# First half's routing and tables inside the last chunk of a scan

## The chip, the cores and the metric

The kernel runs on one core of one Trainium2 chip. The metric is the device time in microseconds of one execution; less is better. Engines are named as in the profile: PE is TensorE (matmuls), PEld its weight loads, DVE VectorE, ACT ScalarE, POOL GpSimd, SP the engine whose queue issues most DMA transfers. Each engine works through its own instructions in their order.

## What is computed

The program is a network of two layers over N = 4096 tokens (rows) with D = 256 features; each layer is a graph step with a residual and then a mixture of experts with a residual. The change touches layer 0 only:

```python
# layer 0, graph step: propagation, layer norm, a Mamba block
h = relu(adj @ layernorm(x) @ gcn_w + gcn_b);  h = layernorm(h) * ln_g + ln_b
xz = h @ w_in;  xc, z = xz[:, :512], xz[:, 512:]
u = silu(causal_conv4(xc));  dt = softplus(...);  B, C = ...   # from u @ w_xp
hst = exp(dt * A) * hst + dt * B * u          # scan over the 4096 tokens, 16 states
y = (hst @ C + u * D_skip) * silu(z)
x = x + y @ w_out
# layer 0, experts: 8 experts of 256 -> 512 -> 256, the two best of each token
n = layernorm(x);  probs = softmax(n @ gate_w + gate_b);  top2 of probs
x = x + sum over the two of  prob * (gelu(n @ W1[e] + b1[e]) @ W2[e] + b2[e])
```

Layer 1 is another graph step and another mixture of experts (6 experts, three matmuls each); its code is the same before and after.

## The kernel before

**The scan.** The tokens are cut into NC = 8 chunks of 512. A chunk is scanned in STEPS = 32 steps; a step works on one block of 128 of the 512 inner channels (`m`) and two of the 16 states. A `Step` does this: POOL multiplies `db` (L1138), ACT makes the two decays `da` with Exp (L1154), DVE runs two scans (L1161) and the product `hc` (L1171), PE adds `hc` into the PSUM tile `psy` (L1188), and after the eighth step of a block DVE multiplies `psy` by the gate (L1197, `us`). The `da` tiles lie in PSUM. The order of the work on PE, DVE, ACT and POOL is written out by hand, within `tc.manual_schedule`: one loop over n = 0 to 255, with chunk c and step i, lists what stands at each step. Each engine therefore works strictly in the order of this loop.

**What is filled in between the steps.** The propagation and the front (projection, convolution, dt) of later chunks fill PE in earlier chunks. In the last two chunks the finished chunks are closed:

- A `Tail` is a half chunk of `y @ w_out + x`: `product(0)` and `product(1)` on PE (L929, L933), `put` (a copy on ACT with row sums, L938, and a store to DRAM, `x1d`), and in the following step `squares` on ACT (L948, L952). `Tail.step` does one such piece at each step, from step 8 of chunk 6.
- A `Norm` is a chunk's layer norm: `root` (POOL's pow, L968), `shift` on DVE (L974), then a fetch, `normal` on ACT with stores to `d_xd` and, for the first four chunks, `xd0`, the transposes (`turn`), the matmuls with `gate_w` (`logits`) and `keep`, which puts the router's logits into `lgs`. The tables `NORMS` and `NPIECES` give the step of the last chunk at which each stands: chunk c's `normal` is at step 10 + 3c.
- `Last` is the last chunk's own tail. Half of its w_out products, the residual and the two banks `ps_out` are begun at steps 22 to 28; the rest (L1063) follows the last gate, and then `norm` (L1077 to L1112) does the statistics, the pow, the normal, the stores, the transposes (L1097), the logits (L1104) and the copies `xr` (L1110).

**Routing.** `dp` is the dispatch of layer 0. The tokens are routed in blocks: b = 0 is the first half (chunks 0 to 3), b = 1 and b = 2 are the rest. `choose` calls `router` (L110 to L138: softmax and the best two, 18 operations on DVE and an Exp on ACT). `place` counts with two matmuls (L231, L235) and turns the counts into row numbers on DVE (L240 to L266). `one_hot` writes comparisons of 128 x 1024 (L273). `Part.tables` then builds the tables of a part: a head of small operations (L311 to L351), pairs `tb_eq` (L359, L364 on DVE, L363 on ACT), 32 products on PE into `ps_inv` (L369), and from these, on DVE, which token lies in which row (`d0f_src`, L381 to L387), which expert a tile has (`d0f_exps`, L389) and the biases (`d0f_b`, L395, L400).

**Expert tiles.** Rows are worked off in tiles of 256 rows of one expert. `part0[0]` has FIRST0 = 9 tiles with rows of the first half of the tokens only; `part0[1]` has the other 26. For a tile, `expert_tiles` gathers rows by two indirect DMAs on POOL (L430, `xk`), loads the expert's weights through SP (`wk`, L532, and `bk`, L535), transposes on PE (L539, `ps_xt`), copies (L543, `xkT`), does the first layer (L518, `ps_h`), the Gelu on ACT (L522), the second layer of the tile before it (L503, `ps_y`), and writes the rows back. `others` is a generator with the routing of blocks 1 and 2 and the tables of the second part; `then0(n)` takes pieces of it after tile n.

**The passage from scan to tiles.** After the last step the loop's end reads, in order: the remaining sums, the last gates, the last additions of `Last`, then

```python
        dp.lo = onehots
        dp.choose(0, lgs[:, :dp.T[0], :], gate_b, False, ra)
        dp.place(0, ps_y, "psy", ra)
        last.norm()
```

and after the pools have been changed

```python
            b1 = load(wp, a["L0_ffn_b1"], "b1")
            dp.one_hot(0)
            for _ in part0[0].tables(inverse(), rp, [b1], NT):
                pass
```

Both blocks stand outside `manual_schedule`; there the order on an engine is that of a scheduler. In the trace before, DVE's router operations on the first half lie between the last chunk's late steps, although they are written after them. The one-hots lie in the first half of `gn`, a large SBUF tile whose rows are not needed at that time.

Of the kernel before, what the change touches and what calls it, by code (L numbers as in the profile page):

```python
# [30 lines left out]
def kernel(ctx: ExitStack, tc: tile.TileContext, out: bass.AP, **a):  # L31
# [73 lines left out]
    def router(ps, bias_b, E, rev, renorm, oh, wv, pool):  # L105
# [4 lines left out]
        nc.vector.tensor_tensor(lg, ps, bias_b.unsqueeze(1).to_broadcast([P, T, E]), ALU.add)  # L110
# [8 lines left out]
        nc.scalar.activation(lg, lg, AF.Exp)  # L119
        nc.vector.tensor_reduce(col(1), lg, AX.X, ALU.add)  # L120
# [6 lines left out]
        for i in range(2):  # L127
# [6 lines left out]
            if i == 0:  # L134
                nc.vector.scalar_tensor_tensor(lg, hots[0], -4.0, p, ALU.mult, ALU.add)
                q = lg
        if not renorm:
# [25 lines left out]
    class Dispatch:  # L163
# [47 lines left out]
        def choose(self, b, logits, bias_b, renorm, pool):  # L211
            T, t0 = self.T[b], self.t0[b]
            hots = self.oh[b][:, 1:, :].rearrange("p (t i) e -> p t i e", i=2)
            router(
                logits, bias_b, self.E, self.rev[:, :T, :], renorm, hots,
                self.wv[:, t0:t0 + T, :], pool,
            )

        def place(self, b, psum, tag, pool):

# [6 lines left out]
            if (2 * G + 1) * E <= CW:  # L227
                tot = ps[:, G * E:]
            else:
                tot = psum.tile([P, CW], F32, name="ps_pl1", tag=tag)  # L230
# [6 lines left out]
            )  # L237
            flat = pool.tile([P, E * (G + 1)], F32, name=f"pl_at{G}")
# [15 lines left out]
            )  # L254
            row = pool.tile([P, G], F32, name=f"pl_row{G}")
# [13 lines left out]
        def one_hot(self, b):  # L269

            g0, G, S, row = 2 * self.t0[b], 2 * self.T[b], 2 * TPC, self.row.pop(b)
            for g in range(0, G, S):
# [3 lines left out]
                )  # L276

    class Part:
# [14 lines left out]
        def tables(self, ps, tp, biases, NG, other=None, hots=None):  # L293
# [4 lines left out]
            if hots is None:  # L298
                def hots(shape):
                    return tp.tile(list(shape), BF16, name="tb_eq", bufs=3)  # L300
# [52 lines left out]
            S = 2 * TPC  # L353
            group = dp.group.rearrange("p t i -> p (t i)")
            slots = slot.rearrange("p f h -> p (f h)").unsqueeze(1).to_broadcast([P, S, C])
            for g0 in range(0, NG, S):
# [11 lines left out]
                for g in range(S):  # L368
                    nc.tensor.matmul(  # L369
                        ps[:, :2 * C], dp.lo[:, g0 + g, :], eq[:, :2, g, :],  # L370
                        start=(g0 + g == 0), stop=(g0 + g == NG - 1),
                    )
# [121 lines left out]
    def expert_tiles(jobs, psum, pool, weights, bias_out, layers, kb_out, also=None):  # L494
# [16 lines left out]
        def layer(w, xT, mb, func, bias, name):  # L511
            hT = pool.tile([P, mb, TR], F32, name=name)
            for mm in range(mb // 2):
                ps = ps_h.tile([P, 2, TR], F32, name="ps_h")
                for j in range(2):
                    m = 2 * mm + j
                    for d in range(DB):
                        nc.tensor.matmul(  # L518
                            ps[:, j, :], w[:, d, m * P:(m + 1) * P], xT[:, d, :],
                            start=(d == 0), stop=(d == DB - 1),  # L520
                        )
                    nc.scalar.activation(hT[:, m, :], ps[:, j, :], func, bias=bias[:, m])  # L522
            return hT

        def tile_of(dp, k, prev):
            e = dp.expert(k)
            xk = pool.tile([P, 2, D], F32, name="xk", bufs=4)
            dp.fetch(k, xk)
# [8 lines left out]
            for d in range(DB):  # L537
                for j in range(2):
                    nc.tensor.transpose(  # L539
                        ps[:, d, j * P:(j + 1) * P], xk[:, j, d * P:(d + 1) * P], ident  # L540
                    )
            hT = pool.tile([P, DB, TR], F32, name="xkT")
            nc.vector.tensor_copy(hT, ps)  # L543
# [6 lines left out]
        prev = None  # L550
# [35 lines left out]
    onehots = gn[:, :NT // 2, :].bitcast(BF16).rearrange("p a (b c) -> p (a b) c", c=P)  # L586
    early = ExitStack()
    ra = early.enter_context(tc.tile_pool(name="route0a", bufs=1, side="right"))
    with ExitStack() as s1:
# [430 lines left out]
        SLOW = 3  # L1020
        NORMS, NPIECES = {}, {}
        for i, c0, c1 in ((1, 0, 3), (13, 3, 5), (19, 5, 6), (25, 6, 7)):
            NORMS[i] = lambda s0=c0 * TPC, n=(c1 - c0) * TPC: Norm.root(s0, n)
            NORMS[i + 1] = lambda s0=c0 * TPC, n=(c1 - c0) * TPC: Norm.shift(s0, n)
        for c in range(NC - 1):
            nm = Norm(c)
            for d, piece in (
                (-2, nm.fetch), (0, nm.normal), (1, nm.turn), (2, nm.logits), (3, nm.keep)
            ):
                NPIECES.setdefault(10 + 3 * c + d, []).append(piece)  # L1030

        class Last:
# [13 lines left out]
            def first(self, hh):  # L1046

                self.ps[hh] = (ps_pt, ps_a)[hh].tile(
                    [P, 2, D], F32, name=f"ps_out{hh}", tag=("pt", "d2")[hh]
# [18 lines left out]
            def norm(self):  # L1068
# [3 lines left out]
                xn, xT = [], []  # L1072
                ps_l = ps_m.tile([P, TPC, E0], F32, name="ps_lg", tag="m1")
                for hh in range(2):
# [11 lines left out]
                    for j in range(2):  # L1086
                        nc.scalar.activation(
# [3 lines left out]
                    nc.sync.dma_start(tokens(dp.xd, c)[:, t0:t0 + 2, :], xn[:, :2, :])  # L1091
                    ps_t = (ps_m if hh == 0 else ps_a).tile(
                        [P, DB, HW], F32, name="ps_xnT7", tag=("m0", "d0")[hh]
                    )
                    for k in range(DB):
                        for j in range(2):
                            nc.tensor.transpose(  # L1097
                                ps_t[:, k, j * P:(j + 1) * P], xn[:, j, k * P:(k + 1) * P], ident
                            )
                    xT = w1p.tile([P, DB, HW], F32, name="xnT7", tag=("h", "hT")[hh])  # L1100
                    nc.scalar.copy(xT, ps_t)
                    for j in range(2):
                        for k in range(DB):
                            nc.tensor.matmul(  # L1104
                                ps_l[:, t0 + j, :], xT[:, k, j * P:(j + 1) * P], gate_w[:, k, :],
                                start=(k == 0), stop=(k == DB - 1),
                            )
                    done = nc.scalar.copy(lgs[:, s0:s0 + 2, :], ps_l[:, t0:t0 + 2, :])
                for hh in range(2):
                    after(nc.scalar.copy(self.xr[hh], self.ps[hh]), done)  # L1110
                    rows = tokens(x1d[c], 0)[:, 2 * hh:2 * hh + 2, :]
                    nc.sync.dma_start(rows, self.xr[hh])  # L1112

        class Step:
# [28 lines left out]
            def decay(self, j):  # L1143
# [4 lines left out]
                if not last or tag != "d2":  # L1148
# [50 lines left out]
        with tc.manual_schedule(engines={  # L1199
# [73 lines left out]
            advance(left)  # L1273
            steps, tails, kept, gated, summed, owed = [], [], {}, [], 0, 0
            for n in range(NC * STEPS):
# [46 lines left out]
                Tail.step(tails)  # L1322
                if c == NC - 1:
# [7 lines left out]
                    elif i == 25:  # L1331
                        last.first(0)
                    elif i in (27, 28):
                        last.residual(i - 27)
# [460 lines left out]
```

## Time and profile before

| | us |
|---|---|
| three runs | 2400.75, 2398.1, 2402.75 |
| median | 2400.75 |
| profiled execution | 2412.49 |
| its span, first to last instruction | 2410.7 |
| PE busy | 2239.3 (93%) |
| DVE busy | 1648.1 (68%) |
| ACT busy | 1194.8 (50%) |
| last chunk: end of its first hc to end of its last hc | 1108.19 to 1246.86 |
| last w_out addition ends | 1255.98 |
| first ps_h product of the tiles begins | 1286.92 |

The mean granted TensorE clock was 0.968 of full speed. Times of the profile count from the first instruction of the span. A row of the timeline gives start, duration, engine, line, operation, and in brackets the idle time before it with what ended it ("<-"). Counts of PE records are those of the trace; a float32 matmul leaves more than one.

### The profile page before, as it was taken

How to read it: one execution, taken by the hardware profiler on the slowest of the kernel's cores; microseconds unless marked ns; L12 is line 12 of the kernel's file. 1: busy time of each engine (PE TensorE's matmuls, PEld its weight loads, DVE VectorE, ACT ScalarE, POOL GpSimd, SP SyncE). 2: the span in 40 equal slices, each digit the busy share in tenths (PEclk: the TensorE clock that was granted, in tenths of full speed). 3: DMA queues.
4: the chain of work that ended last, by engine and by line, in shares of the span. 5: the costliest groups of instructions: out<-in, count | busy, mean ns of one | idle time of the engine just before them, and what ended most of it. 6: DMA issues, size and time to landing. Idle time of an engine off the chain costs nothing. (4 is left out here: it accounts for less than half of the span.)

```text
span 2410.7 us, 28097 instructions
## 1 busy us (share of the span) xinstructions
PE 2239.3 (93%) x9018; PEld 1624.2 (67%) x9018; DVE 1648.1 (68%) x2455; ACT 1194.8 (50%) x2050; POOL 1144.8 (47%) x828
## 2 busy tenths in 40 slices
PE   8999999999999999896997999799999999999985
PEld 7665665656465665553666888667888888877774
DVE  2069999999999999998986411291666667742233
ACT  4255666574655666574753322145555555532321
POOL 1057777777877787775644555310000000045652
PEclk9999999999999999998997999999999999999998
DMA  7279999999999999996848877551444444456786
GB/s 237 83 228 227 241 275 238 274 243 268 247 260 258 238 274 238 271 269 174 270 136 266 295 231 228 162 166 53 143 146 148 146 145 146 148 170 209 230 274 235
DMA packets 293071, 511.58 MB, mean 212 GB/s; under 512 B 25376, under 2 KB 159648, under 8 KB 292016
## 3 DMA queue, kind: packets, MB, share of 16 engines
q1 hardware_dynamic: 246640, 412.64, 54.5%
q0 software_dynamic: 46272, 97.03, 18.7%
q8 instruction: 75, 1.23, 0.2%
q14 instruction: 84, 0.69, 0.1%
HBM read 406.03 MB, written 44.83 MB: 187 GB/s over the span
## 5 line engine op out<-in xcount | busy, mean ns | idle before, releaser
L1138 POOL TENSOR_TENSOR db<-du,bb 128x1024 f32<-128x1024 f32 x256 | 607.1, 2372 | 329.5 <-DVE hc L1171 83.1
L1161 DVE TENSOR_TENSOR_SCAN db<-da,state,db 128x512 f32<-128x512 f32 x512 | 627.2, 1266 | 31.5 <-ACT da L1154 29.3
L671 PE MATMUL pt<-at,gn 128*128 128x256 f32 x2048 | 479.4, 387 | 14.9 <-ACT gn L87 9.2
L671 PEld LDWEIGHTS pt<-at,gn 128*128 128x128 f32 x2048 | 397.1, 195 | 135.7 <-issue 63.1
L1154 ACT ACTIVATE da<-dt,negA 128x512 f32<-128x512 f32 x512 | 346.4, 688 | 249.5 <-DVE db L1161 238.7
L1516 PE MATMUL pf<-gn,f 128*128 128x256 f32 x2048 | 452.0, 380 | 0.0
L1516 PEld LDWEIGHTS pf<-gn,f 128*128 128x128 f32 x2048 | 386.6, 190 | 57.2 <-issue 6.4
L1171 DVE TENSOR_TENSOR hc<-db,cb 128x1024 f32<-128x1024 f32 x256 | 328.0, 1281 | 18.2 <-issue 0.4
L1188 PE MATMUL psy<-hc,ident 128*128 128x512 f32 x576 | 301.6, 618 | 4.6 <-DMA hc<-hc 3.7
L81 POOL TENSOR_TENSOR ln_rs<-ln_rs,mhalf 128x4 f32<-128x4 f32 (+1 forms) x25 | 33.4, 1335 | 507.6 <-DVE ln_rs L80 507.1
L508 DVE TENSOR_TENSOR yk<-ps_y,bk 128x512 f32<-128x512 f32 x73 | 50.4, 691 | 308.9 <-PE ps_y L503 232.2
L1505 ACT ACTIVATE f<-f 128x1024 f32<-128x1024 f32 x128 | 134.6, 1057 | 198.7 <-DVE f L1504 128.2
L518 PE MATMUL ps_h<-xkT,wk 128*128 128x256 f32 x864 | 213.6, 388 | 14.7 <-DVE xkT L543 6.9
L503 PE MATMUL ps_y<-wk,hk 128*128 128x256 f32 x864 | 213.3, 382 | 9.2 <-ACT hk L522 6.6
L1175 POOL DMA_DIRECT2D hc<-hc x224 | 195.0, 870 | 0.2
L518 PEld LDWEIGHTS ps_h<-xkT,wk 128*128 128x128 f32 x864 | 159.1, 192 | 50.6 <-ACT hk L522 11.3
L1504 DVE TENSOR_SCALAR f<-at 128x1024 f32<-128x1024 f32 x128 | 88.1, 688 | 148.0 <-PE pf L1516 134.4
L503 PEld LDWEIGHTS ps_y<-wk,hk 128*128 128x128 f32 x864 | 161.9, 191 | 32.7 <-ACT hk L522 8.4
L1188 PEld LDWEIGHTS psy<-hc,ident 128*128 128x128 f32 x576 | 109.3, 196 | 90.2 <-issue 64.0
L1511 DVE SCALAR_TENSOR_TENSOR cnt<-at,cnt 128x1024 bf16<-128x1024 f32 x120 | 145.9, 1216 | 15.9 <-DMA at<-in_adjT_dram 12.3
L1506 ACT ACTIVATE f<-f 128x1024 f32<-128x1024 f32 x128 | 134.5, 1055 | 3.4
L787 PE MATMUL ps_xz<-hT,w_in 128*128 128x512 f32 x256 | 116.3, 597 | 15.2 <-ACT hT L771 8.8
(321 smaller groups left out, 2513.6 us busy)
## 6 DMA issues: line engine op xcount, KB each, us to landing
at<-in_adjT_dram SPq DMA_DIRECT2D x256, 512.0 KB
bb<-bcd SPq DMA_DIRECT2D x128, 512.0 KB
cb<-bcd SPq DMA_DIRECT2D x128, 512.0 KB
hc<-hc POOLq DMA_DIRECT2D x224, 256.0 KB
wk<-in_L_ffn_W_dram SPq DMA_DIRECT2D x70, 512.0 KB
wk<-in_L_ffn_expert_w_dram SPq DMA_DIRECT2D x114, 256.0 KB
yg<-d_ys SPq DMA_DIRECT2D x14, 512.0 KB
yd<-us SPq DMA_DIRECT2D x6, 1024.0 KB
```

The lines of the kernel that those rows point to most:

```text
L503: nc.tensor.matmul(ps[:, j, :], hT[:, m, j * P:(j + 1) * P], w[:, m, :], start=(m == 0), stop=(m == kb_out - 1),)
L518: nc.tensor.matmul(ps[:, j, :], w[:, d, m * P:(m + 1) * P], xT[:, d, :], start=(d == 0), stop=(d == DB - 1),)
L671: nc.tensor.matmul(pt[:, k, :], xl[:, j, k * P:(k + 1) * P], at[:, jj, :], start=(j == 0 and k == 0), stop=(j == NT - 1 and k == DB - 1),)
L1138: nc.gpsimd.tensor_tensor(self.db, self.f.du[self.half][:, self.mi:self.mi + 1, :].to_broadcast([P, 2, CW]), self.bb, ALU.mult,)
L1154: nc.scalar.activation(da, self.f.dt[self.half][:, self.mi, :], AF.Exp, scale=negA[:, self.m, n:n + 1])
L1161: nc.vector.tensor_tensor_scan(self.db[:, j, :], da, self.db[:, j, :], state[:, self.m, n:n + 1], ALU.mult, ALU.add,)
L1171: nc.vector.tensor_tensor(self.hc, self.db, self.cb, ALU.mult)
L1175: nc.gpsimd.dma_start(self.hc[:, 0, :], self.hc[:, 1, :], accum_op=ALU.add)
L1188: nc.tensor.matmul(f.psy[m], ident, self.hc[:, j, :], start=False, stop=(self.g == GS - 1 and j == last),)
L1505: nc.scalar.activation(f, f, AF.Square)
L1511: nc.vector.scalar_tensor_tensor(cnt, at, 0.0, cnt, ALU.is_gt, ALU.add)
L1516: nc.tensor.matmul(pf[:, t, :], f[:, jj, t * P:(t + 1) * P], gn[:, j, :], start=(j == 0 and t % 2 == 0), stop=(j == NT - 1 and t % 2 == 1),)
```

## The change

- **Where routing stands.** `router`, `place`, `one_hot` and `tables` become generators (`choosing`, `placing`, `one_hots`). `first_half` strings the first half's routing together, and from step 20 of the last chunk on each step takes one piece: the router at steps 20 to 22, the placing matmuls at 24, their DVE work at 25 and 26 with the table's head, one-hots and `tb_eq` pairs at 27 to 30, and all 32 products at 31 (`held`).
- **First rows.** Right after the last `hc` DVE makes the source rows and experts of the table, and POOL gathers the rows of the first two tiles into the second half of `gn` (`Carve` cuts tiles out of it, the held `tb_eq` too). This stands ahead of the last gates and additions. `expert_tiles` takes these tiles from `ready`.
- **Room in the chunk.** `TAILS` does two Tail pieces at each of steps 24 to 31 of chunk 6 and none at steps 0 to 3 of chunk 7. Norm pieces of chunks 0 to 3 stand at 10 + 2c, and the first `root` takes four chunks' columns instead of three.
- **The last norm.** Its transposes, logits and copies of logits go. Its stores of `d_xd` and `x1d` move from SP's to ACT's queue. The rows of the last chunk are read back from `d_xd` (`xn7`, 512 KB) through SP, ahead of the tiles' weights, and `logits7` does the transposes and logits among the first tiles, ahead of the routing of block 2.
- **Among the tiles.** `then0` takes four pieces after each of tiles 1 to 6, where it took three after tiles 0 to 6. The order of the PSUM pools is turned, and PE's first transposes are tied to the first matmul of an earlier tile. `Last`'s second half takes bank `d0`, not `d2`, and its `first(0)` is at step 26, not 25.

Core of the diff:

```diff
+        TAILS = {(NC - 2, i): 2 for i in range(24, STEPS)}
+        TAILS.update({(NC - 1, i): 0 for i in range(4)})
-        for i, c0, c1 in ((1, 0, 3), (13, 3, 5), (19, 5, 6), (25, 6, 7)):
+        for i, c0, c1 in ((1, 0, 4), (13, 4, 5), (19, 5, 6), (25, 6, 7)):
...
-                NPIECES.setdefault(10 + 3 * c + d, []).append(piece)
+                i = (10 + 2 * c if c < NC // 2 else 10 + 3 * c) + d
+                NPIECES.setdefault(i, []).append(piece)
...
-                    nc.sync.dma_start(tokens(dp.xd, c)[:, t0:t0 + 2, :], xn[:, :2, :])
-                    ps_t = (ps_m if hh == 0 else ps_a).tile(
...
-                    done = nc.scalar.copy(lgs[:, s0:s0 + 2, :], ps_l[:, t0:t0 + 2, :])
+                    nc.scalar.dma_start(tokens(dp.xd, c)[:, t0:t0 + 2, :], xn[:, :2, :])
...
-                    nc.sync.dma_start(rows, self.xr[hh])
+                    nc.scalar.dma_start(rows, self.xr[hh])
+
+        def first_half(biases):
+
+            yield from dp.choosing(0, lgs[:, :dp.T[0], :], gate_b, False, ra)
+            yield
+            yield
+            yield from dp.placing(0, ps_pt, "pt", ra, (ps_m, "m0"))
+            table = part0[0].tables(
+                lambda: ps_m.tile([P, CW], F32, name="ps_inv", tag="m0"),
+                room, biases, NT, held=True,
+            )
+            next(table)
+            yield
+            for _ in dp.one_hots(0):
+                next(table)
+                yield
+            yield from table
...
-                Tail.step(tails)
+
+                for _ in range(TAILS.get((c, i), 1)):
+                    Tail.step(tails)
...
+                    if i >= 20:
+                        next(firsts)
...
+            next(firsts)
+            ready = [room.tile([P, 2, D], F32, name="xk", bufs=2) for _ in range(2)]
+            for k, xk in enumerate(ready):
+                part0[0].fetch(k, xk)
             for k in gated:
                 steps[k].gate()
             for m in range(H, MB):
                 for hh in range(2):
                     last.add(hh, m)
-        dp.lo = onehots
-        dp.choose(0, lgs[:, :dp.T[0], :], gate_b, False, ra)
-        dp.place(0, ps_y, "psy", ra)
         last.norm()
...
-            dp.one_hot(0)
-            for _ in part0[0].tables(inverse(), rp, [b1], NT):
+            b1s.append(b1)
+            for _ in firsts:
                 pass
 
+            def logits7(xn):
+                xT = rp.tile([P, 2, DB, HW], F32, name="xnT7", bufs=1)
+                for hh in range(2):
+                    ps = inverse().rearrange("p (k t) -> p k t", k=DB)
+                    for k in range(DB):
+                        for j in range(2):
+                            nc.tensor.transpose(
+                                ps[:, k, j * P:(j + 1) * P],
+                                xn[:, 2 * hh + j, k * P:(k + 1) * P], ident,
+                            )
+                    nc.scalar.copy(xT[:, hh], ps)
+                    yield
...
             def others():
 
+                xn = rp.tile([P, TPC, D], F32, name="xn7", bufs=1)
+                nc.sync.dma_start(xn, tokens(dp.xd, NC - 1))
                 for b in (1, 2):
+                    if b == 2:
+                        yield from logits7(xn)
                     t0 = dp.t0[b]
-                    dp.choose(b, lgs[:, t0:t0 + dp.T[b], :], gate_b, False, rp)
+                    dp.choose(b, lgs[:, t0:t0 + dp.T[b], :], gate_b, False, rp, turned[0])
...
-                if n < FIRST0 - 2:
-                    for _ in range(3):
+                if 0 < n < FIRST0 - 2:
+                    for _ in range(4):
                         next(pieces, None)
```

## The prediction, made before the result was known

> **What bounds the kernel now.** I read the page's busy table first, then the table of 25 us stretches around the end of layer 0's scan, then timelines engine by engine. The page gives the whole:
>
> ```profile
> PE 2239.3 (93%) x9018; PEld 1624.2 (67%) x9018; DVE 1648.1 (68%) x2455; ACT 1194.8 (50%) x2050; POOL 1144.8 (47%) x828
> L1161 DVE TENSOR_TENSOR_SCAN db<-da,state,db 128x512 f32<-128x512 f32 x512 | 627.2, 1266 | 31.5 <-ACT da L1154 29.3
> L1171 DVE TENSOR_TENSOR hc<-db,cb 128x1024 f32<-128x1024 f32 x256 | 328.0, 1281 | 18.2 <-issue 0.4
> ```
>
> PE is nearly full overall, so a gain must come from one of its few gaps. The scan's pace belongs to DVE: two scans and one product take 2.45 + 1.23 = 3.69 us a step. The stretches (columns: PE, PEld, DVE, ACT, POOL busy, granted clock, DMA share, GB/s) show the one large gap:
>
> ```profile
> 1175.00:1200.00 25.00, 25.00 (x115) 17.82 (x114) 24.66 (x23) 16.79 (x48) 17.05 (x8) 0.99 0.91 295
> 1200.00:1225.00 25.00, 25.00 (x114) 17.49 (x113) 23.68 (x29) 19.05 (x53) 15.22 (x8) 1.00 0.82 269
> 1225.00:1250.00 25.00, 23.81 (x92) 15.31 (x91) 21.79 (x27) 12.40 (x28) 10.35 (x5) 0.86 0.31 92
> 1250.00:1275.00 25.00, 14.23 (x80) 9.98 (x78) 18.57 (x87) 7.65 (x18) 1.78 (x2) 0.72 0.27 86
> 1275.00:1300.00 25.00, 16.25 (x62) 12.58 (x63) 11.53 (x59) 6.02 (x10) 12.02 (x12) 0.67 0.71 234
> 1300.00:1325.00 25.00, 25.00 (x153) 21.09 (x152) 20.99 (x60) 10.49 (x20) 13.37 (x12) 1.00 1.00 330
> ```
>
> Until 1243 PE and DVE are both full, with almost no idle time on either. From 1300 the expert tiles fill PE. Between them PE's timeline reads:
>
> ```profile
> 1252.36 3.62 PE L1063 MATMUL ps_out<-w_out,us 128*128 128x256 f32 x16
> ...
> 1276.40 0.39 PE L231 MATMUL ps_pl<-d_oh,tri 128*128 128x128 bf16 x1 [4.42 <-DVE d_oh L133]
> 1276.61 0.42 PE L235 MATMUL ps_pl<-d_oh,ones_b 128*128 128x136 bf16 x1
> 1283.01 0.48 PE L539 MATMUL ps_xt<-ident,xk 128*128 128x128 f32 x1 [5.98 <-DMA xk<-d_xdf,d0f_src]
> ...
> 1286.92 5.02 PE L518 MATMUL ps_h<-xkT,wk 128*128 128x256 f32 x12
> ```
>
> From the last add (1255.98) to the first tile product (1286.92) are **30.9 us**. What ends last is the gather of the first tile's rows; POOL issues it when DVE has finished the tables:
>
> ```profile
> 1276.34 1.18 POOL L430 DMA_INDIRECT xk<-d_xdf,d0f_src  x1 [15.75 <-DVE d_oh L133]
> ```
>
> Early in the same chunk DVE stands still for 7.83 + 2.15 + 1.79 = 11.8 us at steps 7 to 9:
>
> ```profile
> 1132.11 1.22 DVE L1171 TENSOR_TENSOR hc<-db,cb 128x1024 f32<-128x1024 f32 x1
> 1141.16 2.46 DVE L1161 TENSOR_TENSOR_SCAN db<-da,state,db 128x512 f32<-128x512 f32 x2 [7.83 <-ACT da L1154]
> ```
>
> ACT, which works in order, has a Tail's copy ahead of that da; it waits for PE:
>
> ```profile
> 1139.64 0.39 ACT L938 ACTIVATE xr<-ps_out 128x256 f32<-128x256 f32 x1 [5.45 <-PE ps_out L933]
> ```
>
> **What the skill says.** (1) "TensorE: Matmul & The Clock Gate", section "What's actually happening": the array falls to half clock after an idle window of about 3.4 us, and regains it after as long a busy one. The trace agrees: clock 0.72 and 0.67 in the gap, and 12 ps_h records take 5.02 us, where 16 take 3.62 later. (2) "DMA: Bandwidth & Descriptors", "Anatomy of one DMA — SWDGE (gpsimd) path": some 2 us of a DMA are fixed, mostly the confirmation that the last byte is written. Stores of x1d here let their reader go 2.3 us after issue (1164.62 to 1166.91); I use 2.3. (3) "ScalarE: Activation LUTs", "What ACT_TABLE_LOAD costs": 1.28 us a load and more with the drain; the trace shows 1.28.
>
> **The change part by part.** T_h is the end of the last hc (1246.86), T_add that of the last add (1255.98).
>
> *Chunk 6.* Eight more Tail steps stand in steps 24 to 31. On PE they bring six products of about 2.2 us each (13 us; L929 with L933 lasts from 1133.41 to 1135.57), on ACT a copy of 1.0 (L938) and squares of 1.4 (L948, L952) for each Tail. ACT is busy there without a break from 1070.08 to 1092.98, and DVE already waits for da. A copy, squares and a product now stand ahead of da of steps 27 and 28: 1.0 + 1.4, and 1.7 of waiting for the second product that a copy needs and that now comes only in the same step, = **+4.1** (2 to 5), and nothing later in the chunk gives it back. The first Norm root takes 16 columns for 12: POOL's pow took 3.25 for 12, 0.24 a column, so **+0.95** ahead of step 2.
>
> *Steps 0 to 9 of the last chunk.* Four Tail steps go, so ACT no longer waits at 1139.64 for a backlog on PE. PE itself starts some 5 us later (1121.86 to 1126.9), so only about 4 of the 11.8 us are saved: at step 9 the scan is +4.1 + 0.95 − 4 = **+1**. Bound: nothing saved +5, all saved −6.7.
>
> *Steps 10 to 20.* Norm pieces of chunks 0 to 3 come two steps apart, not three. From 1126.9 PE has 71 to 74 us of queued work up to the logits of chunk 3, so they come at about 1201.5; the router at step 20 waits for them, DVE is in order, and step 21's scans stand behind it: **+2.2** (0 to +5) for all that went before, in place of the +1.
>
> *Steps 20 to 31.* All extras are on DVE, which has no slack. From step 20 to 31 it took 45.5 us, 11 × 3.69 = 40.6 and 4.9 of extras. Now: router 18 operations of 0.31, 5.6; placing (L240 to L266) 4.0; table head (L311 to L351) 3.3; one-hots L273 4.62; L359 and L364 four times 0.53, 2.2; the Norm remainder 0.4; together 20.1, thus **+15.2**. ACT's share (Exp, four L363 of 0.41) and PE's two placing matmuls (1.25) lie beside. So T_h' = T_h + 17.
>
> *End of the scan.* 32 table products (16 took 0.70 us, so 1.4) stand ahead of the last psy; PE is only half busy in the last steps. Full clock gives T_h' + 5.7, half +10.3; I take 7.5, before 9.1: T_add' = T_add + **15** (+6 to +22).
>
> *The gap.* Source indices follow on DVE right after the last hc; gathers issued by POOL ahead of the pows land at T_h' + 8 to 12, before or just after T_add', and bind nothing. Next late are the weights, behind SP's queue: the norm chain 5.0 after T_add' (before 6.4, with the placing's DVE work in between), ACT's store of d_xd seen after 2.3, then SP, in order: the reload of xn7 (512 KB), at, b, the exps register, wk: 2.1 for issues. wk leaves at +9.4 and lands, after 1 MB of others at some 350 GB/s, at **+13.2**, where 30.9 was: **−17.7**. Transposes (0.9 a tile half) fit beside. Between 11 (weights land at once) and 20 (the store seen late).
>
> *The tile stage.* It fills PE, so all put into it is added: 8 transposes 1.04, 16 logit records 1.85, placing of block 1 0.8: **+3.7** (3 to 6, if turns cost bubbles). Two table loads, 2.56 on ACT, are costed at nothing: ACT is busy 10.5 of 25 us there. The moved piece pace (four from tile 1) leaves 4 us before the second part's gathers need it; without that cover PE would wait the difference.
>
> Sum: +15 − 17.7 + 3.7 = **+1.0 us**. The profiled execution takes 2412.49 (span 2410.7), 11.7 over the median of the runs, 2400.75; with +1.0 it is 2413.5, and the median **2401.8**.
>
> **Rivals.** *A, the chunk absorbs its load.* The stall at steps 7 to 9 goes wholly and PE's shorter queue gives the router its logits in time. For it: 11.8 us of stall and 13 us of PE work gone from the chunk. Against: the stall is moved PE lateness. T_add' = +7; 7 − 17.7 + 3.7 = −7: 2393.8.
> *B, DVE and a cold PE.* Chunk 6's ACT congestion (+5), the router's wait (+3) and the half clock in the last psy (+4.6 over full) pile up in the in-order scan: T_add' = +22, 22 − 17.7 + 3.7 = +8: 2408.8. It decides against the change from T_add' = +18.8 on. For it: DVE is at 24.66 of 25 us, and the granted clock was 0.50 from 1235 to 1240 already, with PE busy. Against: PE was the later engine before.
> *C, SP's head of the queue.* xn7 waits for ACT's two stores and everything for the tiles queues behind; 7 us late, the gap gives −11: +7.7, 2408.5. Before, wk left at 1270.85, well before the gathers, so nothing shows it.
> *D, it does not do what it says*: the eq tables come late from ACT, products hold psy behind them on PE, rows land after the weights: +4 to +6 more, about 2407.
>
> **How the numbers follow.** 0.2%, 4.8 us, is about what a measurement of this kernel can tell from no change. The sum as worked, within that: 0.32 (2397 to 2406.5 its own range). A: 0.32. B 0.22, C 0.08, D 0.06, together 0.36. The bounds: the low end takes T_add' +6 with a gap of 11 and 3 in the tiles, 6 − 20 + 3 = −11, 2389.8; the high end +22 − 14 + 4.5 = +12.5, 2413. Range 2389 to 2413.
>
> **What would show it.** In the profile after: the da wait at steps 7 to 9 at about 8 us; steps 20 to 31 at 60 to 61 us; last psy to last add short; the first ps_h about 13 us after the last add with wk, not xk, as its releaser; tiles' stage 3 to 6 us longer. Under A the scan ends less than 10 us later; under B more than 19; under C ps_h comes 20 us after the last add. I am wrong if DVE waits for logits more than 5 us at step 20, or if the first tile still waits for gathers.

## The result, and the profile after

The changed kernel takes **2437.39 us** (median of 4 runs, 2432.06 to 2440.96); the kernel before took 2401.31 beside it. The ratio is 1.0150, 95% interval 1.0129 to 1.0172: 36 us slower, where the forecast was 2401.8 and 2413 the upper end of its range.

The page of the changed kernel, the lines that answer to those shown of before (all line numbers are now those of the changed kernel: L1161 became L1232, L1171 became L1242):

```profile
PE 2246.1 (92%) x9018; PEld 1630.1 (67%) x9018; DVE 1668.2 (69%) x2455; ACT 1200.9 (49%) x2051; POOL 1148.1 (47%) x828
L1232 DVE TENSOR_TENSOR_SCAN db<-da,state,db 128x512 f32<-128x512 f32 x512 | 627.5, 1267 | 37.3 <-ACT da L1225 30.5
L1242 DVE TENSOR_TENSOR hc<-db,cb 128x1024 f32<-128x1024 f32 x256 | 327.7, 1280 | 18.3 <-issue 0.3
```

The counts of work hardly moved; DVE is 20 us busier with the same 2455 instructions, PE, ACT and POOL only by 3 to 7 us. That is the first sign that instructions of DVE got longer, and not more. The stretches of 25 us (PE, PEld, DVE, ACT, POOL busy, granted clock, DMA share, GB/s):

```profile
1200.00:1225.00 25.00, 16.59 (x45) 8.16 (x45) 24.48 (x28) 9.81 (x26) 13.61 (x6) 0.85 0.56 177
1225.00:1250.00 25.00, 16.80 (x52) 9.87 (x50) 22.91 (x43) 9.14 (x19) 11.61 (x5) 0.75 0.44 144
1250.00:1275.00 25.00, 14.28 (x44) 9.38 (x44) 24.59 (x30) 8.78 (x19) 9.60 (x3) 0.73 0.12 43
1275.00:1300.00 25.00, 16.11 (x84) 11.02 (x84) 16.44 (x51) 6.59 (x15) 8.35 (x9) 0.78 0.16 48
1300.00:1325.00 25.00, 13.40 (x52) 11.16 (x53) 5.20 (x25) 7.16 (x11) 4.77 (x5) 0.67 0.94 308
1325.00:1350.00 25.00, 25.00 (x133) 21.41 (x132) 18.33 (x67) 9.63 (x18) 12.08 (x12) 1.00 1.03 325
```

Before, PE worked only 14 to 16 of 25 us in two such stretches, from 1250 to 1300; now it works 13 to 17 of 25 in five, 125 us. DVE is nearly full in the first three. I cut the trace of each kernel into stages by five kinds of instruction: starts of `hc` (step 23 of chunk 6, and steps 0, 9, 20, 31 of the last chunk), the end of the last w_out addition, the first `ps_h`, the first `pf` of layer 1. ("Last hc" in the table is the start of `hc` of step 31.) A run's own offset cancels in such differences.

| stage | before | after | difference | as forecast |
|---|---|---|---|---|
| chunk 6, step 23, to last chunk, step 0 | 46.99 | 50.65 | +3.7 | +4.1 |
| steps 0 to 9 | 48.96 | 44.99 | −4.0 | −3.1 |
| steps 9 to 20 | 44.16 | 49.58 | +5.4 | +1.2 |
| steps 20 to 31 | 45.54 | 75.39 | **+29.9** | +15.2 |
| last hc to last addition | 10.35 | 11.37 | +1.0 | −1.6 |
| last addition to first ps_h (the gap) | 30.94 | 18.24 | −12.7 | −17.7 |
| first ps_h to first pf (the tiles) | 296.2 | 306.9 | +10.7 | +3.7 |
| sum | 523.1 | 557.1 | +34.0 | +1.8 |

The forecast terms, as they stand in the prediction, sum to +1.8; it rounded on the way and came to +1.0.

From the first to the last pf, layer 1 takes 544.6 and 545.9. After that the profiled execution of before took 283.0 us, the changed kernel 270.9 and the first eight experiments about as much (268.0 to 272.9). That accounts for the 11.7 us by which that execution stood over its median, and it lies in code that the change doesn't touch. So the stages give the 34, not the difference of the two spans, 24.6.

The largest difference, steps 20 to 31, shows in DVE's timeline of the changed kernel and in POOL's of the same microseconds:

```profile
1214.31 0.26 DVE L125 RECIPROCAL rt_red<-rt_red 128x16 f32<-128x16 f32 x1
1214.60 2.11 DVE L127 TENSOR_TENSOR rt_p<-rt_lg,rt_red 128x128 f32<-128x128 f32 x1
1216.74 0.29 DVE L133 TENSOR_REDUCE rt_red<-rt_p 128x16 f32<-128x128 f32 x1
...
1255.18 1.22 DVE L293 TENSOR_TENSOR gn<-iota,pl_row 128x1024 bf16<-128x1024 f32 x1
1256.31 2.45 DVE L414 TENSOR_TENSOR gn<-gn,d_hi 128x144 bf16<-128x144 f32 x1
```

```profile
1214.22 2.34 POOL L1209 TENSOR_TENSOR db<-du,bb 128x1024 f32<-128x1024 f32 x1 [3.92 <-DVE hc L1242]
...
1255.41 3.20 POOL L1209 TENSOR_TENSOR db<-du,bb 128x1024 f32<-128x1024 f32 x1 [7.68 <-ACT xnT L1076]
```

The like of L127 in the trace before is L123:

```profile
1221.25 0.29 DVE L123 TENSOR_TENSOR rt_p<-rt_lg,rt_red 128x128 f32<-128x128 f32 x1
```

L127 lasts 2.11 us and not 0.29, and ends 0.15 us after POOL's `db` ends at 1216.56. L414 lasts 2.45 for 0.30 and ends 0.15 after the db, which ends at 1258.61. This db itself lasts 3.20 and not 2.34: L293 had begun first, and the 0.86 us more are about what was left of it. So in these rows one of the two engines waits for the other's whole instruction, and who comes first goes first. The Trainium skill, "SBUF — State Buffer", section "Who interferes with whom", says just this: a DVE instruction with two inputs in SBUF contends with a GpSimd instruction that reads SBUF, through a shared port that is held for a whole instruction. The single-input L125 ran beside the first of these two db instructions and kept its 0.26.

The gap in PE's timeline, and what SP issued ahead of the first tile's weights:

```profile
1289.74 3.62 PE L1136 MATMUL ps_out<-w_out,us 128*128 128x256 f32 x16
...
1311.60 9.44 PE L578 MATMUL ps_h<-xkT,wk 128*128 128x256 f32 x32 [16.22 <-DVE gn L453]
```

```profile
1300.49 0.37 SPq L1485 DMA_DIRECT2D xn<-d_xd  x1
1301.21 0.37 SPq L1606 DMA_DIRECT2D at<-in_adjT_dram  x1
1301.69 0.41 SPq L63 DMA_DIRECT2D b<-in_L_ffn_b_dram  x1
1302.85 1.42 SPq L597 DMA_DIRECT2D wk<-in_L_ffn_W_dram  x2
```

The first ps_h is put down to a DVE operation on `gn` (L453) that was long done. What comes last is the landing of wk, issued at 1302.85: ps_h begins 8.75 us later, and the loads of wk in that stretch whose landing the trace shows took 8.5 to 9.1 us.

### The profile page after: what moved, and what is told of

The parts are those of the page before. It is cut to its first block, busy times and chain, and to the rows that moved or that the text cites. A ratio compares the mean times of both kernels' runs of the same rounds, so it can differ in the third digit from the quotient of the medians.

```text
span 2435.3 us, 28082 instructions
## 1 busy us (share of the span) xinstructions
PE 2246.1 (92%) x9018; PEld 1630.1 (67%) x9018; DVE 1668.2 (69%) x2455; ACT 1200.9 (49%) x2051; POOL 1148.1 (47%) x828
## 3 DMA queue, kind: packets, MB, share of 16 engines
HBM read 406.55 MB, written 44.83 MB: 185 GB/s over the span
## 5 line engine op out<-in xcount | busy, mean ns | idle before, releaser
L1232 DVE TENSOR_TENSOR_SCAN db<-da,state,db 128x512 f32<-128x512 f32 x512 | 627.5, 1267 | 37.3 <-ACT da L1225 30.5
L1242 DVE TENSOR_TENSOR hc<-db,cb 128x1024 f32<-128x1024 f32 x256 | 327.7, 1280 | 18.3 <-issue 0.3
L1613 ACT ACTIVATE f<-f 128x1024 f32<-128x1024 f32 x128 | 134.7, 1058 | 212.7 <-DVE f L1612 148.3
L563 PEld LDWEIGHTS ps_y<-wk,hk 128*128 128x128 f32 x864 | 161.4, 191 | 21.7 <-ACT hk L584 0.9
```

What stands on the lines that cost most here:

```text
L563: nc.tensor.matmul(ps[:, j, :], hT[:, m, j * P:(j + 1) * P], w[:, m, :], start=(m == 0), stop=(m == kb_out - 1),)
L1232: nc.vector.tensor_tensor_scan(self.db[:, j, :], da, self.db[:, j, :], state[:, self.m, n:n + 1], ALU.mult, ALU.add,)
L1242: nc.vector.tensor_tensor(self.hc, self.db, self.cb, ALU.mult)
L1613: nc.scalar.activation(f, f, AF.Square)
```

## The experiments

Each was timed beside the kernel before; "over before" is its ratio to it, less one, times 2400 us. One stage table serves the first eight:

| kernel | chunk 6 | 0 to 9 | 9 to 20 | 20 to 31 | end | gap | tiles | ratio, 95% interval |
|---|---|---|---|---|---|---|---|---|
| before | 46.99 | 48.96 | 44.16 | 45.54 | 10.35 | 30.94 | 296.2 | 1 |
| after | 50.65 | 44.99 | 49.58 | 75.39 | 11.37 | 18.24 | 306.9 | 1.0150, 1.0129–1.0172 |
| pieces before product | 50.65 | 45.80 | 49.86 | 57.81 | 12.07 | 18.06 | 304.7 | 1.0084, 1.0069–1.0100 |
| repack only | 50.64 | 44.83 | 49.95 | 42.23 | 8.73 | 31.27 | 295.1 | 1.0005, 0.9998–1.0013 |
| weights first | 50.63 | 45.29 | 48.56 | 75.39 | 11.76 | 3.95 | 314.5 | 1.0113, 1.0098–1.0129 |
| logits in norm | 50.64 | 45.77 | 50.05 | 75.40 | 11.42 | 19.27 | 296.2 | 1.0099, 1.0083–1.0114 |
| pieces and logits | 50.64 | 45.06 | 49.97 | 57.85 | 10.76 | 19.89 | 295.9 | 1.0028, 1.0016–1.0040 |
| stores off SP | 49.93 | 45.19 | 46.81 | 57.85 | 10.75 | 18.87 | 306.6 | 1.0069, 1.0054–1.0084 |
| pieces and weights | 50.63 | 45.06 | 49.29 | 57.84 | 10.77 | 3.65 | 313.1 | 1.0033, 1.0020–1.0047 |
| all four | 49.23 | 45.81 | 46.75 | 57.83 | 10.76 | 9.29 | 299.4 | 0.9984, 0.9976–0.9992 |

### Routing pieces between scans and product

```diff
+                if c == NC - 1 and i >= 20:
+                    next(firsts)
                 cur.product()
...
-                    if i >= 20:
-                        next(firsts)
```

> Edit: the changed kernel, but in steps 20 to 31 of the last chunk the routing piece stands between the step's two scans and its product hc, no longer behind hc. POOL's next db starts when hc ends and lasts 2.35 us, about as long as the two scans, so here POOL is done when the piece begins. Theory A (port): the stretched DVE operations of the changed kernel (L121 2.07, L127 2.11, L134 2.41, L261 1.09, L278 1.56, three L414 of 2.45 us, against 0.15 to 0.30 for their like elsewhere) wait for POOL's db, which reads SBUF at the same time; 14.5 us of them go, steps 20 to 31 take 59 to 63 us in place of 75.4, and the whole is 12 to 15 us shorter than the changed kernel's 2437, about 2423 to 2426. Rival B (the operations are slow for their own sake: strided or broadcast operands, or tiles carved out of gn while DMA writes there): durations stay, steps 20 to 31 stay at 74 to 76 us, 2436 to 2439. Rival C (PE or ACT late): the operations get short but waits for da or ps_pl take their place, less than 5 us gained.

Measured: 2418.19 us, 20 over before where the changed kernel was 36 over it; theory A, with about one us more than it said. The same operations in its DVE timeline:

```profile
1208.35 0.26 DVE L125 RECIPROCAL rt_red<-rt_red 128x16 f32<-128x16 f32 x1
1208.64 0.29 DVE L127 TENSOR_TENSOR rt_p<-rt_lg,rt_red 128x128 f32<-128x128 f32 x1
...
1242.31 0.29 DVE L414 TENSOR_TENSOR gn<-gn,d_hi 128x144 bf16<-128x144 f32 x1
```

Nothing but the place changed, and 2.11 and 2.45 us became 0.29; DVE's busy time falls from 1668.2 to 1652.0 us with the same 2455 instructions. Steps 20 to 31 take 57.8, which is 17.6 less: 14.5 are the stretched operations, 1.4 a wait for ps_pl that is gone too (DVE waited for it at step 25), 1.7 I did not trace to single operations. What is left over before, 12.3, is the work itself; the forecast of that stage, +15.2, was 2.9 too high even for a place where POOL is at rest.

### The repack alone

The `TAILS`, `NORMS` and `NPIECES` lines of the diff, on the kernel before.

> Edit: the kernel before, with the changed places of Tail and Norm pieces alone (two Tail pieces at steps 24 to 31 of chunk 6, none at 0 to 3 of chunk 7, Norm of chunks 0 to 3 two steps apart, first root of 16 columns). Routing, tables, last norm and tiles stay as before. Theory A: this part costs by itself what the changed kernel shows ahead of step 20 (hc of step 20 was 6.5 us later there, 1.4 of it already at step 1040 us): about +4 in chunk 6, nothing at steps 0 to 9, +4.6 at step 17, where POOL waits for bb, whose load stands on SP behind the stores of a Norm piece. The router has then less PE work in its way, but DVE sets the pace: +4 to +7 us on the before kernel, 2405 to 2408. Rival B (the repack pays for itself, as PE has less behind step 10 and the last psy come sooner): -3 to +1, 2398 to 2402.

Measured: 2400.24, +1.2 us (−0.5 to +3.1), no difference that can be told. The parts of theory A are all there (chunk 6 +3.7, steps 9 to 20 +5.8, with a wait of 3.8 for POOL's db), and so is what theory A left out: steps 0 to 9 −4.1, steps 20 to 31 −3.3 and the end −1.6. Part of the −3.3 are router operations, the last of which now fall behind the last hc, where the gap hides them. Rival B holds: the repack costs nothing by itself.

### Weights first

```diff
-                nc.sync.dma_start(xn, tokens(dp.xd, NC - 1))
+                after(nc.sync.dma_start(xn, tokens(dp.xd, NC - 1)), begun[0])
...
+                if c == 0 and j2 < 4:          # ld: layer 1's load of at
+                    after(ld, begun[0])
```

> Edit: the changed kernel, with the loads of xn7 and of the first four at tiles of layer 1 tied behind the first ps_h matmul of tile 0, so that on SP the first tile's weights stand behind nothing that waits for the last norm. Theory A (SP's queue, and the burst of loads it lets out at once): in the changed kernel wk left at 1302.85, 14.7 us after the experts' numbers were ready, and took 9.1 us to land; here it leaves within 4 us of the last addition or before it, the first ps_h comes 3 to 8 us after the last addition in place of 18.2, and the whole is 8 to 13 us shorter than 2437: 2424 to 2429. Rival B (the gathers or xkT bind next): the first ps_h stays 14 us or more behind. Rival C (the time is given back, as the second tile's weights and the at tiles come later): first ps_h early, whole less than 4 us shorter.

Measured: 2425.21, about 9 us less than the changed kernel by the ratios. The gap falls from 18.2 to 3.95, and the tiles give 7.6 of it back. Its PE timeline shows where:

```profile
1293.90 3.30 PE L578 MATMUL ps_h<-xkT,wk 128*128 128x256 f32 x8
1301.42 8.16 PE L578 MATMUL ps_h<-xkT,wk 128*128 128x256 f32 x24 [4.22 <-DMA wk<-in_L_ffn_W_dram]
```

Theory A holds in every number, and a part of rival C came as well: SP's queue did hold the first weights back, and behind it the second tile's weights are next. SP issued these at 1295.22 and 1296.96; the second falls together with the landing of the last norm's store of d_xd, issued at 1294.07 and landed some 2.9 us later.

### Logits back in the last norm

The changed kernel without `logits7` and the reload; `norm` has again its transposes, copy and logits.

> Edit: the changed kernel, with the last chunk's transposes and logits back in the last norm (stores stay on ACT's queue), no reload of xn7, and none of its pieces among the tiles. Theory A: among the tiles these cost their PE time, 3.1 us (transposes 1.2, logits 1.9), and part of the waits for hk and xkT that the crowded DVE and ACT bring (7.4 us in the changed kernel, 2.0 before); in the gap they lie beside the wait for the weights. First ps_h to the first pf of layer 1 is 4 to 8 us shorter than the changed kernel's 306.9, the gap from last addition to first ps_h within 3 us of 18.2, the whole 3 to 8 us shorter than 2437. Rival B (the gap grows by what the tiles lose, since wk's buffer waits for the logits): 2435 to 2440.

Measured: 2422.23, 12 us less than the changed kernel by the ratios (8.5 by the stages), more than expected. The tiles take 296.2, exactly what they took before, so the whole +10.7 of that stage came with these pieces and the reload of xn7; the two were not taken apart. 3.1 us are the PE work of the pieces. PE's waits over the tiles, of the changed kernel and then of this one:

```profile
PE ps_h L578 <- ACT hk L584: 4.3, 2, 2.6
PE ps_h L578 <- DVE xkT L611: 3.1, 2, 2.4
```

```profile
PE ps_h L578 <- DVE xkT L611: 1.8, 1, 1.8
```

These waits are 7.4 us in the changed kernel, 1.8 here and 2.0 before. What stood behind the longest of them in the changed kernel:

```profile
1355.24 0.69 DVE L1612 TENSOR_SCALAR f<-at 128x1024 f32<-128x1024 f32 x1 [2.57 <-DMA at<-in_adjT_dram]
1355.97 1.06 ACT L1613 ACTIVATE f<-f 128x1024 f32<-128x1024 f32 x1 [7.11 <-DVE f L1612]
1357.44 3.55 PE L578 MATMUL ps_h<-xkT,wk 128*128 128x256 f32 x8 [2.61 <-ACT hk L584]
```

DVE, in its order, waited for a load of layer 1's adjacency (`at`), ACT's L1613 waited for DVE, and the Gelu (at 1356.93) stood behind L1613. Two of the other three waits, at 1387.01 and 1396.21, also follow a DVE operation that waited for `at`; together the three are 6.7 of the 7.4 us. After the wait these 8 records of ps_h take 3.55 us, where 8 take 1.89 in the tiles around it. The routing of block 2 brings two table loads of 1.28 us among the tiles' Gelus in the changed kernel (at 1336.08 and 1337.65), and they are gone here; but no wait of PE stands beside them.

### Two edits at a time

> Edit: both at once, the routing pieces between scans and product, and the last chunk's logits back in the last norm (no reload, nothing of it among the tiles). Theory: the two losses lie in different stages and add up. From the stages of the single edits: steps 20 to 31 take 57 to 59 us, first ps_h to first pf 296 to 298 us (304.7 with the pieces alone), the gap 18 to 20; against the pieces alone (18.6 us over the before kernel) 7 to 10 us less, so 8 to 12 us over the before kernel, 2408 to 2412. Rival: with the tables earlier the tiles are crowded all the same, and less than 4 us come.

Measured: 2405.15, 6.7 us over before (1.0028), a little below what was expected. By the stages the two edits add up (57.85 and 295.9).

> Edit: the routing pieces between scans and product, and the loads of xn7 and of layer 1's first at tiles behind tile 0's first ps_h. Theory: additive again. The gap is 4 to 6 us in place of 18.1, and 6 to 8 us are given back among the tiles, since the second tile's weights leave SP only when the stores of the last norm are done (wk waited for 4.2 us when this edit stood alone); 7 to 10 us less than the pieces alone, so 8.5 to 12 over the before kernel. Rival: nothing is given back, then 3 to 5 over it.

Measured: 2406.24, 7.9 over before, again a little below; the gap is 3.65, and the tiles take 313.1: 8.4 given back, as in the single edit (7.6).

### Stores off SP's queue

```diff
-                nc.sync.dma_start(tokens(dp.xd, self.c), self.x)
+                nc.scalar.dma_start(tokens(dp.xd, self.c), self.x)
...
-                    nc.sync.dma_start(tokens(xd0, self.c), self.x)
+                    nc.scalar.dma_start(tokens(xd0, self.c), self.x)
```

> Edit: the routing pieces between scans and product, and the stores of the Norm pieces (d_xd, xd0) issued from ACT's queue instead of SP's. Theory: DVE's wait of 4.6 us at step 17 for POOL's db comes from SP: the load of bb stands there behind a store that waits for ACT's normal. With the stores elsewhere it goes; hc of step 9 to hc of step 20 takes 45 to 46 us in place of 49.6 to 49.9, and the whole is 3 to 5 us shorter than with the pieces alone (18.6 over the before kernel), so 13.5 to 16 over it. Rival A (bb waits for the free buffer or for DMA traffic): the wait stays. Rival B (ACT pays: 0.4 us an issue in its order makes da late): gain under 2 us.

In the changed kernel SP issued the stores of d_xd and xd0 at 1189.68 and 1190.08, when ACT's normal had ended (1189.65), and only then bb; POOL, then DVE waited:

```profile
1192.31 4.66 POOL L1209 TENSOR_TENSOR db<-du,bb 128x1024 f32<-128x1024 f32 x2 [7.58 <-DMA bb<-bcd]
```

```profile
1194.69 2.46 DVE L1232 TENSOR_TENSOR_SCAN db<-da,state,db 128x512 f32<-128x512 f32 x2 [4.59 <-POOL db L1209]
```

Measured here: no wait for POOL is left in DVE's waits of the last chunk, and steps 9 to 20 take 46.8, 3.0 less than with the pieces alone and 0.8 more than expected, as 1.5 us of waits for da stand there now. The time, 2415.94, is 3.6 less by the ratios than with the pieces alone, which the intervals (1.0054 to 1.0084 and 1.0069 to 1.0100) do not separate. That the wait comes from these stores on SP is shown; that the whole is shorter without it is not.

### All of it: the idea without its losses

The edits above together, with the transposed rows of the norm in the free half of `gn`:

```diff
-                    xT = w1p.tile([P, DB, HW], F32, name="xnT7", tag=("h", "hT")[hh])
+                    xT = room.tile([P, DB, HW], F32, name="xnT7", bufs=2)
```

> Edit: all of these: pieces between scans and product, Norm stores on ACT's queue, weights ahead of layer 1's at tiles, logits in the last norm with their transposed rows in the free half of gn, so that no weight buffer waits for them. Theory, by stages against the before kernel: chunk 6 +3.7, steps 0 to 9 -4.0, steps 9 to 20 +1, steps 20 to 31 +12.3, last hc to last addition +1.5, gap 31 to 8 to 10 (PE does the norm's transposes and logits before tile 0), -22, tiles 0 to +3: sum -7.5 to -4.5, 2392 to 2396, the change's idea faster than the before kernel. Rival A (what DVE took on in the chunk is never earned back, the freed gap turns into waits for the second tile's weights or for xk): within 2 us of the before kernel or slower. Rival B (stores on ACT's queue make da late): steps 9 to 20 at 48 us or more.

Measured: **2396.78** beside 2398.98, ratio 0.9984 (0.9976 to 0.9992), 3.8 us faster than before by the ratio (the two medians are 2.2 apart). That is 0.16%, and less than the 4.5 to 7.5 expected. The stages sum to 519.1 against 523.1. PE's way from the last addition to the first tile product:

```profile
1269.17 3.62 PE L1137 MATMUL ps_out<-w_out,us 128*128 128x256 f32 x16
1272.62 1.04 PE L604 MATMUL ps_xt<-ident,gn 128*128 128x128 f32 x8
...
1280.33 1.88 PE L1177 MATMUL ps_lg<-gate_w,gn 128*128 128x8 f32 x8 [0.68 <-ACT gn L1174]
1282.07 3.33 PE L578 MATMUL ps_h<-xkT,wk 128*128 128x256 f32 x7
```

Neither rows nor weights are waited for; the norm's own chain fills the 9.3 us. Of the 21.7 us that the gap loses, DVE's work in steps 20 to 31 takes 12.3 back and the tiles 3.2; the other stages together take 2.1.

### The port by itself

Two operations were added behind (or ahead of) `hc` in each of the 64 steps of chunks 2 and 3 of the kernel before.

> The disputed cost by itself. Edit: the kernel before, with two operations on DVE added behind the product hc of each of the 64 steps of chunks 2 and 3: a tensor_reduce of 128x128 (one SBUF input) and then a tensor_tensor of 128x128 (two SBUF inputs), whose results nobody reads. Theory (port): the first takes 0.25 to 0.3 us; the second comes while POOL's db runs and waits for its end, 2.0 to 2.4 us; the scans start late by both. About 64 x 2.5 = 160 us, less where DVE would have waited anyway: +120 to +160. Rival (such operations are slow only on the operands of the routing, broadcast or strided): both 0.3, +37 or less.

> Edit: as the one before, but both added operations are the tensor_reduce with one SBUF input, in the same place. Theory (port): neither waits though POOL's db runs, 0.25 to 0.3 us each, 64 x 0.6 = +25 to +38 us. Rival (whatever stands there waits for POOL or for a semaphore): the second takes 2 us or more, as with two inputs.

> Edit: the same two operations as in the first of these (tensor_reduce, then tensor_tensor of two SBUF inputs), but between the step's scans and hc, where POOL's db has just ended. Theory (port): 0.25 to 0.3 us each, +25 to +40 us, some 100 us less than behind hc. Rival: two inputs cost 2 us here too, or the product's delay makes POOL's db the later one and DVE waits 1 us or more a step for it.

Before took 2414.65 on that chip. Measured in this order: 2569.76 (ratio 1.0638, 1.0547 to 1.0730), 2441.95 (1.0109, 1.0023 to 1.0196) and 2433.50 (1.0080, 1.0068 to 1.0091), so +155, +27 and +19 us, the last somewhat under the 25 expected. DVE's groups of these operations (count, busy time, mean ns), one fence for each kernel:

```profile
L1314 DVE TENSOR_TENSOR probe<-iota,ident 128x128 f32<-128x128 f32 x64 | 145.7, 2277 | 2.2
L1313 DVE TENSOR_REDUCE probe<-iota 128x1 f32<-128x128 f32 x64 | 17.8, 279 | 0.0
```

```profile
L1314 DVE TENSOR_REDUCE probe<-iota 128x1 f32<-128x128 f32 x64 | 18.3, 286 | 2.2
L1313 DVE TENSOR_REDUCE probe<-iota 128x1 f32<-128x128 f32 x64 | 17.9, 279 | 0.0
```

```profile
L1313 DVE TENSOR_TENSOR probe<-iota,ident 128x128 f32<-128x128 f32 x64 | 19.2, 300 | 2.2
L1312 DVE TENSOR_REDUCE probe<-iota 128x1 f32<-128x128 f32 x64 | 16.8, 262 | 0.0
```

The same operation with two inputs costs 2.28 us behind hc and 0.30 ahead of it; one input costs 0.29 in the bad place too. The mean of 2.28 has two parts: 60 of the 64 began while a db ran and took 2.40 to 2.43 us, the other four 0.29. Operands, semaphores and the mere presence of extra work are excluded.

The one-input operation differs from the other also in its kind and in what it writes (128x1, not 128x128). A trace speaks on this too: a tensor_tensor that writes 128x512, with one of its two inputs in PSUM, ran beside db without a wait. Of the two in the row below, 1.28 us together, the second began within the db (changed kernel). So neither the kind nor the width of what is written brings the wait by itself:

```profile
1004.94 1.28 DVE L806 TENSOR_TENSOR h<-ps_gcn,gcn_b 128x512 f32<-128x512 f32 x2
```

```profile
1005.18 2.35 POOL L1209 TENSOR_TENSOR db<-du,bb 128x1024 f32<-128x1024 f32 x1 [0.41 <-DVE hc L1242]
```

## Why the prediction was wrong, by its own steps

**Steps 20 to 31 is the step that failed.** It counted every operation and took its duration from the before trace, "18 operations of 0.31". There the scheduler had spread the router over many steps, and each of its operations with two inputs began where POOL ran no db, or in the last quarter of a microsecond of one. The change puts them behind hc, where db runs. The price was read without asking what ran beside the row it came from. 29.9 us were measured for +15.2: 14.7 us of the 32.2 by which the stages missed the forecast. And before's trace had shown it:

```profile
1114.17 2.22 DVE L974 TENSOR_TENSOR x_shift<-x_mean,x_dev 128x12 f32<-128x12 f32 x1
```

```profile
1114.02 2.33 POOL L1138 TENSOR_TENSOR db<-du,bb 128x1024 f32<-128x1024 f32 x1
```

This operation on 12 columns with two inputs ended with the db; of the two on 4 columns later on, one took 0.92 us beside a db and the other 0.14 with POOL at rest. The step said that DVE "has no slack" and was right in that, since every us came through.

**The tiles, +3.7 forecast, +10.7 measured.** The PE work of the pieces was right (3.1 of logits and transposes). What failed is "it fills PE, so all put into it is added": 5.4 us are waits that this sum had at nothing, most of them behind late loads of layer 1's adjacency, for which DVE and then ACT stood in their order. The last 2.2 were not traced in full; 1.7 of them are the slow ps_h records after the longest wait. The two table loads, which the prediction did put at nothing, cost PE no wait. A mean share of 10.5 in 25 us on ACT does not tell what stands ahead of a given Gelu.

**The gap, −17.7 forecast, −12.7 measured.** SP's order was read right and wk left 9.5 us after the last addition, where 9.4 was worked out. Its landing was mis-sized: 3.8 us were allowed, and it took about 8.75. Rows, at, xn7 and the later weights were moved in the same microseconds (DMA share 0.94 from 1300 to 1325). Where fewer loads stood around it, a load of this size landed 5.3 us after its issue (weights first) and 4.0 (all four); so sharing is the likely reason, but no run isolates it. Rival C came near in number (−11) by luck: it had SP 7 us late, and SP was on time.

**Steps 9 to 20, +1.2 forecast, +5.4 measured.** The step looked for a wait of the router for its logits; that wait did not occur. 4.6 us came on a queue that the step did not list: the compressed Norm stores held bb back on SP. The end (−1.6 forecast, +1.0) went the other way too: from the end of the last hc to the last addition it took 10.1 us, where 7.5 was chosen between 5.7 at full clock and 10.3 at half. Four psy records ahead of the table products still ran at half clock, 3.76 us where four take 1.88; that is 1.9 of the 2.6.

**Right were** chunk 6 (+4.1, measured +3.7), steps 0 to 9 (−3.1, measured −4.0; its term for the larger pow, +0.95, was 0.63: 3.88 us for 16 columns after 3.25 for 12), and where the gap's next wait would be (wk, not xk). Rival B had the direction: DVE became the bound and the time went over its point of decision, T_add' = +18.8, by far, as the first five stages sum to +36.0. But its reasons, ACT congestion, the router's wait and a cold PE, were not the main ones, so its direction is no credit to it. Rival A's cheap chunk did not come: DVE still waited 7.1 us for da in steps 0 to 9. Of rival D nothing shows: the table products ran without a wait, and the rows came before the weights.

The signs that the prediction named for being wrong, a long wait for logits at step 20 and a first tile that waits for gathers, did not appear either: they watched the waits, and the miss lay in durations. The range failed because its upper end combined only costs that were named. It did not even take the worst of each (+22, −11 and +6 make +17, or 2418), but that would not have reached 2437: the price of an operation in a new place was not bounded from above, though the price beside POOL could be read from L974.

## What to carry to other kernels

A duration read from a profile belongs to a place: before using it for a moved operation, look at what GpSimd does in the old place and in the new one, and keep two-input DVE work out of GpSimd's reads (here ahead of hc, not behind it: 16 us for a line of code). And look at durations, not only at waits: a blocked instruction shows in these traces as a longer one, with no idle time before it. When work is moved to fill a gap, follow each queue past which it moves, SP's above all; here SP held back bb in the chunk and wk in the gap. An idea that loses can be a good idea with separable losses: taken one by one by stages, they turned +36 us into −3.8.

## What the runs showed of the hardware that I had not expected

- A 128x128 tensor_tensor of DVE with two SBUF inputs waits for a running GpSimd tensor_tensor to its end: 2.28 us for 0.30, on average over 64. The rule is the skill's (the page named above); its size here is what is left of the other's 2.34 us, and a little over. The other way round GpSimd's instruction grew from 2.34 to 3.20 us. Not every GpSimd instruction did this: in the trace before, L130 and L131 (two inputs, 0.29 us each, from 1222.98) ran within POOL's pow of 128x4 (1221.70 to 1223.61), and why is open.
- DVE's two scans of 128x512, whose da lies in PSUM, kept 2.45 us beside db throughout, and the tensor_tensor L806 its 0.68: with one of two inputs in PSUM no wait was seen.
- One input does not always spare the wait: a cast from float to int (L278, 128x32) took 1.56 us beside db, for 0.18 ahead of hc, and a scaling (L1035, 128x4) once 1.06 for 0.23. These are single rows of the changed kernel's trace, and no run varies them.
